# A new written order for all engines of a four-layer graph network kernel

## The chip, the cores and the metric

The kernel runs on one core of a Trainium2 chip. The metric is the device time of one execution in microseconds, as the median over runs. Below, PE is TensorE (matmuls), DVE is VectorE, ACT is ScalarE, POOL is GpSimd and SP is SyncE, which only issues DMA transfers.

## The reference

The input x is a batch of 128 matrices of 128 nodes by 512 features in float32; adj is one 128 x 128 matrix. Four layers follow each other, each as x = layernorm(x + layer(x)):

```python
# layer 0
y   = einsum('nm,bmd->bnd', adj, x);  out = y @ weight + bias
# layer 1
q, k, v = x @ Wq.T, x @ Wk.T, x @ Wv.T
rel = adj.T * (q @ k.T);  rel = rel / norm(rel, axis=2);  out = rel @ v
# layer 2
h   = x @ W;  s1, s2 = h @ a1, h @ a2
e   = leaky_relu(s1[:, :, None] + s2[:, None, :]) * adj
out = elu(softmax(e) @ h + beta * h)
# layer 3
pre = (adj @ x)[:, :, None, :] + ((adj @ x + b) - adj @ x)[:, :, :, None]
out = max(relu(pre), axis=-1)
```

## The kernel before, in words

**Groups and stages.** The batch is cut into NG = 32 groups of G = 4 matrices. A group is one tile of 128 partitions x 4 x 512. The layers are pipelined over the groups: while TensorE works on layer 0 of group g (tiles named y), it also works on layer 1 of group g-1 (m, rel, v, o) and layer 2 of group g-2 (z), with layer 3 of the group before that (p_a). In the steady state every period holds the same steps for successive groups.

**The four big products.** In each group there are four products of a [512 x 512] left side with a [512 x 512] weight: y with the weight of layer 0, x with the product of Wq and Wk (m), x with Wv (v), and z with the weight of layer 2. Each is done by the Strassen-Winograd scheme in seven block products instead of eight (`product`, line 533; the products are numbered 1 to 7, `ORDER`, `REGION` and `BLOCK` say in which order, in which PSUM region and for which block). In most groups the block products 2 and 4 are done by the same scheme once more, on 128 x 128 blocks (`inner_product`, line 498), in three steps each: products 1, 2 and 5, then 6 and 3, then 7 and 4 (`SMALL`). Both inner products of one big product share two PSUM banks with tag pi. An inner step writes into a bank only when VectorE has read the earlier step's result of that bank. So there are three kinds of names: r_y, r_m, r_v, r_z are results of plain block products (256 columns a matmul), pi_y, pi_m, pi_v, pi_z those of inner ones (128 columns), and p_y, p_z, p_rel, p_o, p_a are the small products with adj, the attention or the scores.

**Who does what.** The sums of left blocks that the scheme needs, s_y, s_x, s_z for the outer and si_y, si_x, si_z for the inner level, are made by GpSimd (`left_factors`, line 358). The results are added into the tiles x (layer 0), tT (scores), v and c (layer 2) by VectorE, some are copied by ScalarE. Transposes of activations into yT and zT come out of p_y and p_z by ScalarE copies; xT, relT and eT are made by VectorE's block transposes (xB, relB, eB) and DMA transfers on SP's queue. The normalisation (`norm`, line 615) takes statistics on VectorE (`stats`: BN statistics and their aggregation), ve on VectorE, rstd = ve^(-1/2) on GpSimd, nmean on VectorE and the scaling of x by ScalarE. In layer 2, s1 and s2 are dot products on VectorE; s2 goes through DRAM and comes back spread over the partitions (s), and then VectorE makes e<-s,d and the leaky step e<-e, two steps with both operands in SBUF, GpSimd multiplies by adj, VectorE takes the maximum, ScalarE the exponential, VectorE divides and adds beta (four steps).

**What sets the order.** Each step is not run where it is written but recorded with a number:

```python
def emit(at, f, *args):
    pieces.append((at, lambda: f(*args)))
...
for _, f in sorted(pieces, key=lambda p: p[0]):
    f()
```

The steps run in the order of these numbers, and the class InOrder (line 18) keeps each engine's instructions in that order. All instructions are issued from InOrder's helper, so all have line L26 in the profile. A step's number is 28 x group plus a value of `TABLE` (`times`). `FIRST` replaces values for groups 0 and 1 and `LAST` for the last three groups; `STEPS` gives, relative to the start of a big product, when each block product and each inner step begins and when its result is read. The scale is only an order: nothing waits for a point of time. What waits is decided by semaphores, for data and for buffers.

Of the kernel before, what the change touches and what calls it, by code (L numbers as in the profile page):

```python
# [10 lines left out]
ALU = mybir.AluOpType  # L11
# [18 lines left out]
def kernel(  # L30
# [215 lines left out]
    def row(at, step, n=G):  # L246
# [4 lines left out]
        load=[-23.2169], y=[0.4502, 1.7198, 2.5377, 4.2529],  # L251
        y_sums=[5.3577, 5.4124, 7.8235, 8.8388], y_inner=[6.5498, 7.664, 8.3588, 9.0762],
        y_w=[6.7589, 7.6588, 8.3277, 16.9708, 16.9901, 20.5607, 22.7653],
        stats0=[13.328, 13.6989, 14.9332, 14.6913], norm0=[15.5628],
        apply0=[17.0291, 17.8869, 17.7334, 18.253], turn=[16.7073, 16.2021, 14.9969, 20.612],
        turn_blocks=[17.8971, 18.3579, 19.2263, 19.3554],
        move=[20.4296, 21.0211, 24.5297, 21.5216], x_sums=[25.5005, 25.8871, 27.6629, 27.0652],
        x_inner=[27.1832, 28.0762, 28.1744, 27.3808],
        m=[27.6814, 29.311, 30.5193, 32.9685, 32.6007, 32.3909, 36.4113],
        scores=[35.7913, 36.5286, 36.9062, 39.5258], masked=[40.2], squares=[41.6744],  # L260
        turn_rel=[40.7045], move_rel=[40.942, 41.4556, 41.6809, 42.7864], inverse=[42.997],
        v=[41.1715, 38.9562, 41.2808, 38.8925, 41.0631, 48.9771, 50.8054],
        attend=[51.0766, 51.9776, 54.2466, 53.0567], residual=[51.4403, 53.0619, 54.4101, 55.0641],
        squares1=[51.8389, 54.8288, 55.7527, 55.9297], dots=[52.2629, 53.9621, 54.8819, 55.6838],
        norm1=[56.0324], scale=[57.2146], apply1=[65.5539, 65.7375, 66.5847, 65.6302],
        spread=[58.597], leaky=[61.9353], weighted=[63.694], greatest=[63.7], exps=[64.3087],
        divide=[64.7559], turn_att=[67.1344], with_beta=[64.8337], turn_blocks_2=[64.9823],
        move_2=[66.4103], gather=[70.2679, 71.1247, 73.2155, 74.6156],
        z_sums=[75.1661, 76.1025, 77.0322, 77.3655], z_inner=[76.1384, 77.0913, 77.9699, 79.3217],
        z_w=[76.5003, 77.2488, 83.0675, 84.5887, 83.8747, 83.1527, 86.1311],  # L270
        exp=[85.3247, 85.2563, 97.2575, 99.4893], elu=[86.3247, 87.0299, 97.3808, 99.5574],
        norm2=[101.3033], apply2=[101.8904, 102.4013, 101.9063, 102.7223],
        widen=[104.0541, 104.4241, 105.8654, 107.0522],
        top=[104.3944, 105.3458, 106.4158, 107.431], norm3=[107.8979],
        apply3=[108.3981, 108.8547, 108.4952, 109.5013], store=[110.1315],
# [4 lines left out]
            y=[0.3837, 1.3837, 2.675, 3.675], y_sums=[5.7775, 6.2775, 7.2553, 7.6358],  # L280
            y_w=[6.8732, 7.6921, 8.8732, 9.8732, 10.8732, 11.5739, 12.3292],
            stats0=[14.4311, 14.4511, 14.4711, 14.4911], norm0=[15.816],
            m=[27.9566, 28.8805, 29.1757, 30.7027, 31.7537, 33.399, 33.5276],
            scores=[35.8497, 37.2073, 38.2073, 39.2073], masked=[39.9091], squares=[40.2891],
            turn_rel=[40.3993], move_rel=[42.0292, 41.2824, 41.094, 41.4824],
            v=[41.5081, 42.8089, 44.1636, 45.1636, 46.1636, 46.9988, 48.1636],
            attend=[50.6594, 51.5743, 52.6759, 53.6594], residual=[51, 52, 52.7256, 54.3006],
            squares1=[51.1766, 54.1407, 54.0138, 54.8004], norm1=[55.4948],
            apply0=[16.9376, 17.4687, 18.2447, 17.3632], turn=[18.8709, 20.6961, 20.9961, 21.4413],
            dots=[57.8, 58.1728, 59.9, 60.8223], scale=[61.2], spread=[61.7187], leaky=[62.1],  # L290
            weighted=[62.9], greatest=[64.0022], exps=[64.0333], divide=[65.5939],
            turn_blocks_2=[65.6], move_2=[65.65],
        ),
        1: dict(
            y=[-9.5161, -9.1442, -8.9161, -8.6161], y_sums=[-3.9496, -3.8496, -3.7496, -0.3469],
            y_w=[6.782, 7.7109, 8.6136, 9.601, 10.8116, 11.7295, 12.4613],
            stats0=[14.434, 14.5716, 15.1787, 15.3716], norm0=[16.6316],
            attend=[49.7, 52.43, 53.8336, 54.02], apply0=[18.7873, 19.43, 18.9743, 19.0873],
            turn=[20.5431, 20.6, 20.9, 21.2], x_sums=[22.1338, 23.4592, 24.0133, 26.9575],
# [5 lines left out]
            exp=[1.911, 11.611, 13.6093, 22.0992], elu=[5.6806, 13.5806, 18.6837, 22.1806],  # L305
            norm2=[23.3538], apply2=[24.522, 25.322, 26.3798, 26.0092],
            squares3=[34.1015, 35.8608, 35.7015, 37.144],
            widen=[43.9865, 55.4735, 53.8545, 58.1545], top=[45.1541, 57.9003, 58.5754, 60.4402],
            norm3=[64.2098], apply3=[66.5259, 66.9597, 67.9456, 68.5597], store=[69],
        ),  # L310
        NG - 2: dict(
            scale=[4.2], apply1=[4.5, 5.3942, 6.3, 6.1139], spread=[6.9011], leaky=[7.4],
            weighted=[9], greatest=[10.9571], exps=[12.8968], divide=[14.9407], turn_att=[18.5691],
            with_beta=[19.6], gather=[33.3301, 34.4633, 35.0947, 36.2151],
            z_sums=[37.1312, 37.1799, 37.2299, 38.9411],
            z_w=[37.2, 39.2089, 41, 42.6626, 44.8626, 46.5626, 48.2373],
            exp=[50.3972, 50.8866, 52.8866, 55.5591], elu=[52.4416, 54.6916, 59.5187, 64.5381],
            norm2=[65.7882], apply2=[67.872, 68.672, 69.472, 70.2058],
            widen=[73.03, 68.9544, 73.2544, 75.7764], top=[73.9203, 74.6682, 75.9682, 77.4682],
            stats3=[70.2144, 73.2078, 72.4861, 72.0071], norm3=[75.9789],  # L320
            apply3=[78.882, 79.8, 80.9786, 81.3657], store=[85.9721],
        ),
        NG - 1: dict(
            load_w2=[-23.6669], m=[-1.0871, 0.5618, 2.2887, 4.0287, 7.6759, 7.9287, 9.6287],
            scores=[12.8205, 13.6, 14.5, 15.7481], masked=[15.9045], squares=[16.4941],
            turn_rel=[17.4768], inverse=[19],
            v=[16.8753, 18.5753, 20.8511, 22.2355, 24.5079, 25.8571, 28.3688],
            attend=[28.9525, 29.7018, 30.5618, 31.4218], residual=[30.4, 31.27, 32.14, 33.01],
            stats1=[33.9, 34.2915, 34.1, 34.2], norm1=[34.3934],
            dots=[35.0895, 36.4469, 36.5469, 40.2922], scale=[42.7],  # L330
            apply1=[39.4587, 40.2587, 44.5045, 41.8587], spread=[43.4886], leaky=[44.7702],
            weighted=[46.0349], greatest=[48.0816], exps=[48.1871, 48.7343, 49.3109, 49.9109],
            divide=[48.5065, 49.3785, 49.9, 50.5], turn_att=[49.6131, 50.2131, 50.8131, 51.4131],
            with_beta=[49.934, 50.6249, 51.134, 51.6586],
            gather=[50.9668, 52.0102, 55.557, 62.8965], z_w=[52.2222, 56.5222, 60.615, 64.3222],
            exp=[55.264, 59.8536, 64.1536, 67.7536], elu=[55.3119, 60.4986, 66.3119, 69.7119],
            norm2=[57.5244, 62.8236, 67.713, 71.113], apply2=[59.9822, 65.342, 70.78, 74.4822],
            widen=[62.5511, 69.3064, 73.7305, 76.6387],
            stats3=[61.0987, 66.6487, 74.0987, 75.9582], norm3=[62, 67.45, 74.2351, 76.6],
            top=[69.7698, 73.416, 75.4098, 76.9098], apply3=[70.5171, 74.3, 76.4, 78],  # L340
            store=[73.5499, 75.2, 76.6055, 78.2055],
# [76 lines left out]
    def by_columns(p, a, b, first):  # L418

        for c in range(2):  # L420
            for k in range(2):
# [19 lines left out]


    STEPS = {
        "m": (
            {
                1: (0.0547, 0.3858),
                6: (1.5064, 1.6818),
                7: (2.8763, 2.9047),
                5: (4.4211, 5.0801),
                3: (5.9851, 6.5109),  # L450
            },
            {
                2: ((1.231, 1.341), (2.5246, 2.879), (4.1971, 4.3926)),
                4: ((4.0286, 4.2384), (5.2415, 5.786), (6.8079, 8.6144)),
            },
        ),
        "0": (
            {
                1: (-0.2799, 0.7512),
                6: (1.3262, 1.5837),  # L460
                7: (3.3936, 3.4058),
                5: (4.5192, 5.2093),
                3: (6.2408, 6.2609),
            },
            {
                2: ((0.7436, 1.3293), (2.4284, 2.8511), (4.032, 5.0699)),
                4: ((3.4633, 4.0434), (5.1574, 5.9066), (6.5107, 6.8625)),
            },
        ),
# [802 lines left out]
```

## Time and profile before

| | |
|---|---|
| median of 3 runs | 2172.33 us (2172.3 to 2172.41) |
| profiled execution | 2172.45 us |
| its span in the trace | 2170.2 us |
| granted TensorE clock | 0.998 |
| PE / DVE / ACT / POOL busy | 98% / 82% / 59% / 45% of the span |
| DMA | 139.67 MB, mean 64 GB/s |

The profile was taken in one execution. The span is what the engines' records cover, the execution's own time is 2.25 us longer. A row of the timeline gives the start, the busy time, the engine, the operation, the tile that is written and the tiles that are read, and in square brackets the idle time of the engine before it with what ended it. A matmul in float32 counts as two records in the trace. The ends of matmuls are modelled from their size, so a row's busy time can overlap the next row's start, and the distance of starts is the better measure.

### The profile page before, as it was taken

Reading aid. Unit: us, or ns where it says so; the run is one execution under the profiler, and the core shown is the slowest. Engines: PE = TensorE matmul, PEld = TensorE weight load, DVE = VectorE, ACT = ScalarE, POOL = GpSimd, SP = SyncE. Lnnn points to the kernel's source line nnn. Section 1 sums busy time; section 2 is a strip of 40 time slices with the busy share of each in tenths; the row PEclk is TensorE's granted clock in tenths of the full one; section 3 lists DMA queues with packets and bytes.
Section 4 is the critical chain, followed back from the end, with each engine's and each line's share of the span. In section 5 each row is a group of like instructions: output and inputs, shape, how many; then the busy total and the mean of one; then the engine's idle time right before and its main releaser. Section 6 shows DMA issues by size and latency. Waiting matters only on the chain.

```text
span 2170.2 us, 36980 instructions
## 1 busy us (share of the span) xinstructions
PE 2123.9 (98%) x12325; PEld 1838.2 (85%) x12325; DVE 1784.4 (82%) x4961; ACT 1289.7 (59%) x2950; POOL 971.8 (45%) x949
## 2 busy tenths in 40 slices
PE   9999999999999999999999999999999999999996
PEld 7788888888888888888888888888888888888883
DVE  5688888888888888888888888888888788888887
ACT  3335566665566665566665566655666655676655
POOL 4244454444454444553544554444544445535431
PEclk9999999999999999999999999999999999999999
DMA  4012232222232222322222322312222213232201
GB/s 171 25 35 50 68 74 69 54 65 57 73 70 74 54 58 60 75 67 66 67 52 67 73 69 54 72 52 71 71 73 54 58 60 76 67 72 61 53 26 59
DMA packets 362526, 139.67 MB, mean 64 GB/s; under 512 B 303200, under 2 KB 318688, under 8 KB 362336
## 3 DMA queue, kind: packets, MB, share of 16 engines
q1 hardware_dynamic: 361808, 136.27, 24.9%
q8 instruction: 98, 1.61, 0.3%
q10 hardware_dynamic: 528, 1.05, 0.1%
q14 instruction: 92, 0.75, 0.1%
HBM read 56.17 MB, written 41.48 MB: 45 GB/s over the span
## 4 chain that ended last, share of the span: by engine, by line
PE 78%; DVE 9%; POOL 9%; issue 2%; ACT 1%; DMA 0%; SPq 0%; DVEq 0%; POOLq 0%; ACTq 0%
PE r_v L26 13%; PE r_z L26 12%; PE r_m L26 10%; PE r_y L26 6%; PE p_z L26 5%; PE p_y L26 5%; PE p_o L26 5%; PE p_a L26 5%; PE pi_v L26 4%; POOL s_y L26 4%; PE pi_z L26 4%; PE pi_m L26 3%; DVE x L26 3%; POOL si_y L26 3%; PE pi_y L26 2%
## 5 line engine op out<-in xcount | busy, mean ns | idle before, releaser
L26 ACT ACTIVATE x<-x,nmean,rstd 128x512 f32<-128x512 f32 x384 | 286.1, 811 | 95.8 <-DVE nmean L26 95.7
L26 ACT ACTIVATE scr<-x 128x512 f32<-128x512 f32 x360 | 225.7, 627 | 131.6 <-DVE x L26 128.8
L26 POOL TENSOR_TENSOR rn<-n,mhalf 128x4 f32<-128x4 f32 x32 | 33.0, 1030 | 374.8 <-ACT sq L26 374.8
L26 POOL TENSOR_TENSOR rstd<-ve,mhalf 128x4 f32<-128x4 f32 (+1 forms) x99 | 98.2, 992 | 228.5 <-DVE ve L26 227.5
L26 DVE SCALAR_TENSOR_TENSOR scr<-x,wa 128x512 f32<-128x512 f32 x256 | 175.0, 684 | 5.6
L26 DVE TENSOR_REDUCE mx<-p_a 128x1 f32<-128x512 f32 x128 | 88.0, 688 | 100.8 <-PE p_a L26 100.8
L26 ACT COPY v<-r_v 128x512 f32<-128x512 f32 x128 | 71.4, 582 | 160.1 <-PE r_v L26 160.1
L26 DVE TENSOR_TENSOR tT<-pi_m,tT 128x128 f32<-128x128 f32 x420 | 121.2, 306 | 54.3 <-PE pi_m L26 47.8
L26 POOL TENSOR_TENSOR s_y<-yT 128x512 f32<-128x512 f32 x32 | 40.6, 1267 | 249.1 <-ACT yT L26 249.1
L26 DVE TENSOR_TENSOR x<-r_y,x 128x512 f32<-128x512 f32 x194 | 129.8, 682 | 19.5 <-PE r_y L26 17.4
L26 PE MATMUL p_a<-x,adjT 128*128 128x512 f32 x256 | 131.8, 601 | 5.9 <-ACT x L26 4.2
L26 PEld LDWEIGHTS p_z<-eT,x 128*128 128x128 f32 x1024 | 131.6, 192 | 6.5 <-DVE x L26 0.8
L26 PE MATMUL p_y<-adjT,x 128*128 128x128 f32 x1024 | 134.5, 275 | 0.4 <-DMA x<-in_x_dram 0.4
L26 PE MATMUL p_z<-eT,x 128*128 128x128 f32 x1024 | 134.8, 275 | 0.0
L26 ACT COPY yT<-p_y 128x512 f32<-128x512 f32 x128 | 74.9, 585 | 100.2 <-PE p_y L26 100.2
L26 DVE TENSOR_TENSOR c<-pi_z,c 128x128 f32<-128x128 f32 x420 | 124.0, 307 | 11.3 <-PE pi_z L26 2.4
L26 PEld LDWEIGHTS p_y<-adjT,x 128*128 128x128 f32 x1024 | 129.1, 192 | 3.8 <-issue 0.5
L26 PE MATMUL p_o<-v,relT 128*128 128x512 f32 x256 | 130.7, 595 | 0.3 <-ACT xT L26 0.2
L26 PEld LDWEIGHTS p_rel<-xT,tT 128*128 128x128 f32 x1024 | 127.0, 192 | 3.4
L26 PE MATMUL p_rel<-xT,tT 128*128 128x128 f32 x1024 | 129.7, 275 | 0.0
L26 DVE TENSOR_TENSOR x<-pi_y,x 128x128 f32<-128x128 f32 x420 | 120.8, 306 | 9.4
L26 DVE TENSOR_TENSOR v<-pi_v,v 128x128 f32<-128x128 f32 x420 | 119.2, 302 | 6.2
(244 smaller groups left out, 6130.9 us busy)
## 6 DMA issues: line engine op xcount, KB each, us to landing
out_dram<-x SPq DMA_DIRECT2D x128, 256.0 KB, 2.1
x<-in_x_dram SPq DMA_DIRECT2D x31, 1024.0 KB, 7.4
xT<-xB SPq DMA_DIRECT2D x480, 64.0 KB, 2.3
relT<-relB SPq DMA_DIRECT2D x496, 16.0 KB, 1.8
eBd<-eB SPq DMA_DIRECT2D x30, 256.0 KB, 2.0
eT<-eBd SPq DMA_DIRECT2D x120, 64.0 KB, 2.0
s<-s2d SPq DMA_DIRECT2D x29, 256.0 KB, 5.2
w_sb<-in_L_gnn_weight_dram ACTq DMA_DIRECT2D x1, 1024.0 KB, 5.9
```

The lines of the kernel that those rows point to most:

```text
L26: return lambda *args, **kw: self.tc.keep_in_program_order(op(*args, **kw))
```

## The change

Only numbers change: the values of `TABLE`, `FIRST`, `LAST` and `STEPS`, and the lists of numbers handed to `emit`, `each`, `weight_blocks`, `left_factors` and `product` at the end of the function. Every engine runs the same instructions as before, in another order, with the same tiles and the same number of buffers. Counted out over a period of the steady state, the largest moves are these:

- p_y of blocks 1 to 3 and their copies into yT come earlier among the m products; the last r_m and pi_m pieces of group g-1 then follow them.
- GpSimd's order of a group's left sums is: s_y, s_y, si_y, then e x adj, yT, s_y, si_y, yT, si_y (before: s_y, s_y, si_y, si_y, e x adj, yT, si_y, s_y, yT). VectorE's e<-s,d and leaky step come after the first three.
- The inner steps and block products of y, m, v and z interleave differently (`STEPS`), so also the reads on VectorE.
- rstd of layer 1 moves behind the x sums on GpSimd. In the statistics of layer 0, block 3's come before block 2's as they did, with other steps between; nmean of layer 2 stands directly behind the step that GpSimd's rstd waits for (before, five adds of v stood between), as nmean of layer 0 stood and stands behind its own, apart from two adds of v.
- GpSimd's z sums run s_z, s_z, zT, si_z (before: s_z, s_z, si_z, zT).
- In the first groups the preparation of weights is placed anew, and products 7, 4, 3 of group 0 replace 7, 3, 4. In the last three groups the order of VectorE's, ScalarE's and TensorE's steps is shuffled within a few steps.

```diff
     TABLE = dict(
-        load=[-23.2169], y=[0.4502, 1.7198, 2.5377, 4.2529],
-        y_sums=[5.3577, 5.4124, 7.8235, 8.8388], y_inner=[6.5498, 7.664, 8.3588, 9.0762],
-        y_w=[6.7589, 7.6588, 8.3277, 16.9708, 16.9901, 20.5607, 22.7653],
-        stats0=[13.328, 13.6989, 14.9332, 14.6913], norm0=[15.5628],
-        apply0=[17.0291, 17.8869, 17.7334, 18.253], turn=[16.7073, 16.2021, 14.9969, 20.612],
+        load=[-21.1232], y=[0.9608, 1.8251, 2.1487, 2.7922],
+        y_sums=[4.5561, 5.0639, 6.7629, 6.9969], y_inner=[5.2833, 7.5035, 7.9599, 7.7423],
+        y_w=[6.4865, 10.1067, 9.7011, 18.5098, 16.5578, 25.5346, 18.8593],
+        stats0=[13.0727, 13.9676, 15.6348, 14.8804], norm0=[15.6928],
+        apply0=[16.441, 16.56, 17.1055, 18.4252], turn=[16.9531, 18.9169, 15.0983, 23.7872],
...
-        spread=[58.597], leaky=[61.9353], weighted=[63.694], greatest=[63.7], exps=[64.3087],
-        divide=[64.7559], turn_att=[67.1344], with_beta=[64.8337], turn_blocks_2=[64.9823],
-        move_2=[66.4103], gather=[70.2679, 71.1247, 73.2155, 74.6156],
-        z_sums=[75.1661, 76.1025, 77.0322, 77.3655], z_inner=[76.1384, 77.0913, 77.9699, 79.3217],
+        spread=[61.4852], leaky=[62.1614], weighted=[62.3481], greatest=[63.6868], exps=[63.9389],
+        divide=[64.6743], turn_att=[66.48], with_beta=[55.7842], turn_blocks_2=[65.0697],
+        move_2=[65.6032], gather=[70.1205, 71.0446, 73.2368, 74.4083],
+        z_sums=[74.7466, 74.9675, 75.3471, 79.5091], z_inner=[76.2873, 76.452, 76.7576, 79.7843],
...
-        norm2=[101.3033], apply2=[101.8904, 102.4013, 101.9063, 102.7223],
+        norm2=[100.4793], apply2=[101.1271, 102.2, 101.6434, 101.6261],
...
     STEPS = {
...
         "0": (
             {
-                1: (-0.2799, 0.7512),
-                6: (1.3262, 1.5837),
-                7: (3.3936, 3.4058),
-                5: (4.5192, 5.2093),
-                3: (6.2408, 6.2609),
+                1: (-0.2886, 1.0861),
+                6: (1.2661, 2.3878),
+                7: (3.1719, 4.2315),
+                5: (4.092, 4.8012),
+                3: (5.8133, 6.3959),
             },
             {
-                2: ((0.7436, 1.3293), (2.4284, 2.8511), (4.032, 5.0699)),
-                4: ((3.4633, 4.0434), (5.1574, 5.9066), (6.5107, 6.8625)),
+                2: ((0.925, 1.543), (2.5418, 3.9993), (4.5688, 5.5801)),
+                4: ((3.0391, 3.7075), (5.0748, 5.9439), (6.0353, 6.4062)),
             },
         ),
```

`STEPS` for "m", "v" and "2" and the remaining values of `TABLE`, `FIRST`, `LAST` and the lists at the end change in the same manner.

## The prediction

> **What bounds the kernel now.** I read the page's busy times first, then one window of the steady state, then the waits, then the timelines of TensorE, GpSimd and VectorE around the two places that the waits name. Page, then windows (length, then busy us of PE, PEld, DVE, ACT, POOL):
>
> ```profile
> PE 2123.9 (98%) x12325; PEld 1838.2 (85%) x12325; DVE 1784.4 (82%) x4961; ACT 1289.7 (59%) x2950; POOL 971.8 (45%) x949
> ...
> 1020.00:1088.00 68.00, 67.35 (x402) 59.00 (x401) 57.06 (x166) 42.36 (x98) 31.41 (x31) 1.00 0.25 63
> 2108.00:2170.20 62.20, 43.96 (x155) 25.82 (x153) 50.38 (x144) 34.92 (x67) 14.77 (x17) 0.92 0.13 51
> ```
>
> TensorE sets the pace for all but the last 60 us, where VectorE does (busy 9.3 to 9.4 us in each 10 from 2130 on). Only its gaps can be won. The steady ones are of two kinds only (waits: us in total, times, longest):
>
> ```profile
> PEld pi_y L26 <- POOL si_y L26: 14.5, 29, 0.6
> ...
> PE pi_y L26 <- DVE x L26: 9.7, 29, 0.3
> ...
> PE pi_y L26 <- POOL si_y L26: 8.9, 29, 0.4
> ```
>
> Timeline of TensorE in group 15 (start, busy, count of records; idle before in brackets):
>
> ```profile
> 969.34 0.61 PE L26 MATMUL pi_y<-w_sb,yT 128*128 128x128 f32 x4
> 970.25 0.49 PE L26 MATMUL pi_y<-u,si_y 128*128 128x128 f32 x2 [0.30 <-POOL si_y L26]
> 970.58 1.06 PE L26 MATMUL p_rel<-xT,tT 128*128 128x128 f32 x8
> ...
> 973.20 1.95 PE L26 MATMUL p_rel<-xT,tT 128*128 128x128 f32 x16
> 974.98 0.39 PE L26 MATMUL pi_y<-u,si_y 128*128 128x128 f32 x2
> ...
> 977.60 0.39 PE L26 MATMUL pi_y<-u,si_y 128*128 128x128 f32 x2
> 978.32 0.68 PE L26 MATMUL pi_y<-u,yT 128*128 128x128 f32 x4 [0.33 <-DVE x L26]
> 978.84 1.89 PE L26 MATMUL r_y<-w_sb,s_y 128*128 128x256 f32 x8
> ```
>
> Pitch: 16 records from 973.20 to 974.98 are 0.111 each (a product 128 wide is two records, 0.222; one 256 wide 0.432, one 512 wide 0.86). After 969.34 + 4 x 0.111 = 969.78 the next should start; it starts at 970.25, 0.47 late, and its two records take 0.33 instead of 0.22. The second: due 977.82, starts 978.32, 0.50 late, then 0.52 instead of 0.44. Together 0.47 + 0.11 + 0.50 + 0.08 = 1.16 us per group; the bracketed idle is smaller because ends are modelled. Cross-check: si_y comes 30 times from 113.6 to 2022.1, a period of 65.81 us; one group's products (48 of 0.222; 8 of 0.86; in each of four big products 20 of 0.432 and 14 of 0.222) are 64.6, and 64.6 + 1.16 is that period. So 29 x 1.16 = 33.6 us is all that the steady state can give back.
>
> Why si_y is late, GpSimd and then VectorE:
>
> ```profile
> 967.20 1.86 POOL L26 TENSOR_TENSOR s_y<-s_y,yT 128x512 f32<-128x512 f32 x1
> 969.02 1.17 POOL L26 TENSOR_TENSOR si_y<-yT 128x256 f32<-128x256 f32 x1
> 970.27 0.73 POOL L26 TENSOR_TENSOR si_y<-si_y,yT 128x256 f32<-128x256 f32 x1
> ...
> 966.17 1.81 DVE L26 TENSOR_TENSOR e<-s,d 128x512 f32<-128x512 f32 x1
> 968.01 1.59 DVE L26 SCALAR_TENSOR_TENSOR e<-e 128x512 f32<-128x512 f32 x1
> ```
>
> The same sums elsewhere take 1.27 and 0.73, the e steps at least 1.08 and 0.69: VectorE and GpSimd take turns.
>
> **What the Trainium skill says.** "SBUF — State Buffer", section "Who interferes with whom": a VectorE instruction with two SBUF inputs and a GpSimd instruction that reads SBUF exclude each other for a whole instruction; ScalarE and TensorE have ports of their own. The trace agrees: 1.86 against 1.27, 1.17 against 0.73, 1.81 against 1.08, and steps with a PSUM operand keep their length. "Perfetto Trace Analysis", section "GPSIMD Engine Instruction": spans there are unreliable, starts are to be used. Here the difference is small: s_y 1.27, spacing about 1.35 for the first.
>
> **The change, part by part.** No instruction is added or removed, so the sum is made of waits only. "Matmul time" is TensorE's own time between two points if it never waits, counted from the new order with the pitches above.
>
> *Stall 1.* Before, 4.79 us of matmul time lie between the last p_y and the first pi_y<-u,si_y, and 4.79 + 0.47 = 5.26 was needed. After, p_y of block 3 stands earlier, with its ScalarE copy, and 8.93 lie between; the m products that it overtakes end later, and the scores p_rel, which need them, keep 0.6. Needed without hold-up: eviction 0.3 + 0.58, s_y 1.35 + 1.3, si_y 0.75 = 4.3. Slack 4.6; even held as before it holds. Both e steps of VectorE now follow these sums. Gain 0.47 + 0.11.
>
> *Stall 2.* The third pi_y step reuses the bank of the second. Before, 2.40 us of matmul time lay between, 2.90 were needed; after, 4.13. Gain 0.50 + 0.08. What is late next: VectorE's read of r_y after product 6 now queues behind the reciprocal and the four e steps, which wait for the landing of s (5.2 us). I get a read end 0.1 to 0.2 before product 7 is due; a landing 0.5 later would stall 0.4. GpSimd's last si_y/yT before the second pi_y step has 0.2 to 0.6.
>
> *New waits around norm0.* VectorE's nmean of layer 2 now stands directly behind its ve (before, five v adds lay between), as that of layer 0 stood already behind ve and two v adds; each time VectorE waits up to 1 us for GpSimd's rstd (1.01). Counting VectorE's queue from the last y add in positions of matmul time (r_v's first product at 0): two adds to 1.5, four statistics of 0.8, four x3 steps of 0.69 and three v adds of 0.28 bring ve to 8.4, rstd to 9.5, nmean after it, the second pair to 11.1, xB 0.65, three v adds 0.9: the bank is free at 12.7 to 12.8, and TensorE wants it at 12.7. I take 0.1 plus 0.1 of restart; 0 to 0.6 is open. Behind the second nmean also stand ScalarE's x3 steps and zT copies; the last zT ends at about 15.6, and GpSimd's new order s_z, s_z, zT, si_z (1.35 + 1.25 + 1.25 + 0.75; before, si_z came third) ends at 20.2, TensorE wants si_z at 20.1, 0.2 late with its latency of 0.1; the slip above covers half. I take 0.4 per group for all new waits, 0 below and 1.0 above as bounds.
>
> *Moved without cost.* rstd of layer 1 goes behind all x sums on GpSimd: the x sums gain 1 us, the 16 xT transfers start about 1.4 us later and still land ahead (si_x slack some 3 us). SP's queue keeps its rows; the x load stands 2.1 of 28 slots later, still most of a period ahead of its use. If that cover were gone, m products would wait 1 us per group.
>
> *Start-up.* TensorE's gaps from 10 to 170 us sum to 9.7. Products 7 and 4 go ahead of 3 in group 0, so that two evictions lie beside it (a gap of 1.46 at 61.7 goes); other gaps may grow. I take -2, bounds -5 and +2.
>
> *Tail.* Same VectorE-bound work, shuffled; one nmean there waits 0.6 for rstd, one PE wait of similar size goes. I take 0, bounds -2 and +2.
>
> Sum: 29 x (0.4 - 1.16) = -22, -2, 0: about -24. Profiled execution 2172.45 (span 2170.2 and 2.25 around it), the median 2172.33, so they are interchangeable: 2172.4 - 24 = 2148.5. I predict 2149.
>
> **Rivals.**
> (a) As worked out, 54%: 2142 to 2156 (0.15 to 0.6 of new waits per group).
> (b) The new waits are covered, 22%: 2172.4 - 33.6 - 2 = 2137, 2135 to 2142. For it: TensorE's 29 equal gaps are the only steady ones, and my new ones are within 0.2 of nothing. Against: several have that slack at once.
> (c) A new wait takes the old ones' place, 15%: the chain through both rstd comes 0.8 later than worked out, or the s landing moves the e chain by 0.6 and r_y stalls: 0.9 to 1.1 per group, 2163 to 2172.
> (d) Slower, 9%: VectorE's queue stands behind GpSimd's pow twice, and with it ScalarE's x and zT, GpSimd's z sums. From 1.3 us lateness of that one chain on, what it costs exceeds 1.16 and the 2 us of start-up; at 1.8 it is 29 x 0.6 = +17: 2188. For it: the waits of before already have nmean on rstd 33 times, up to 1.1 us, and ScalarE's x on nmean for 95.7 us in all; against: GpSimd is 45% busy and has nothing else queued there in the new order.
> That the change doesn't do what it says is excluded: the new order of p_y and of the e steps can be counted.
>
> **How the numbers follow.** 0.2% is 4.3 us, about what a measurement can tell from no change. (a), (b) and the lower half of (c), 0.08, are faster; within 0.2% (2168 to 2176.7) falls the upper half of (c), 0.07; (d) is slower, 0.09. The range leaves out the lower end of (b) (0.05), the top of (c) (0.04) and (d): 2136 to 2170; case (a) alone 2142 to 2156.
>
> **What would show it.** Right: no wait of pi_y on si_y or x of 29 times; first s_y sums 1.27 and si_y 0.73; a si_y period of 65.1 (64.6 for b). New rows in the waits, 29 times each, of pi_v on v or pi_z on si_z, and nmean on rstd with two waits of about 1 us per group. Wrong: a period of 65.5 or more, r_y waiting for x, or TensorE waiting for v over 0.6 at a time.

## The result and the profile after

The changed kernel takes 2141.59 us (median of 4 runs, 2141.52 to 2141.63), beside 2172.32 us of the kernel before on the same chip. The ratio is 0.9859, with a 95% interval of 0.9842 to 0.9876: it is faster by 1.4%, or 30.7 us. The forecast was 2149, with a range of 2136 to 2170; the measured time lies just below case (a) (2142 to 2156) and within case (b) (2135 to 2142), at its upper end.

The page of the kernel after, busy times and the chain that ended last, then that chain before:

```profile
PE 2116.7 (99%) x12325; PEld 1836.7 (86%) x12325; DVE 1725.1 (81%) x4961; ACT 1293.5 (60%) x2950; POOL 954.3 (45%) x949
...
PE 94%; DVE 3%; SPq 1%; DMA 1%; POOL 0%; issue 0%; ACT 0%; ACTq 0%; DVEq 0%; POOLq 0%
...
PE 78%; DVE 9%; POOL 9%; issue 2%; ACT 1%; DMA 0%; SPq 0%; DVEq 0%; POOLq 0%; ACTq 0%
```

Before, PE had 78% of that chain, DVE and POOL 9% each. Now it is PE's nearly alone. VectorE's busy time is 59 us smaller (1784.4 to 1725.1) with the same instructions: a step that is held up by a step of the other engine counts as busy in the profile, so a hold-up that goes shows as less busy time, not as less idle time.

The waits view has no row in which pi_y waits for si_y or for x any more. Some waits of the other engines have grown. The one that the prediction named is this (us in total, times, longest; before 21.4, 33, 1.1):

```profile
DVE nmean L26 <- POOL rstd L26: 54.5, 63, 1.1
```

Timeline of group 16's y sums, first GpSimd, then VectorE, then TensorE:

```profile
1010.27 1.71 POOL L26 TENSOR_TENSOR s_y<-yT 128x512 f32<-128x512 f32 x1 [2.99 <-ACT yT L26]
1012.06 1.27 POOL L26 TENSOR_TENSOR s_y<-s_y,yT 128x512 f32<-128x512 f32 x1
1013.29 0.72 POOL L26 TENSOR_TENSOR si_y<-yT 128x256 f32<-128x256 f32 x1
...
1015.40 1.06 DVE L26 TENSOR_TENSOR e<-s,d 128x512 f32<-128x512 f32 x1
1016.50 0.69 DVE L26 SCALAR_TENSOR_TENSOR e<-e 128x512 f32<-128x512 f32 x1
...
1017.97 0.61 PE L26 MATMUL pi_y<-w_sb,yT 128*128 128x128 f32 x4
1018.42 0.39 PE L26 MATMUL pi_y<-u,si_y 128*128 128x128 f32 x2
```

The first si_y starts at 1013.29, is done 0.72 later, and TensorE wants it at 1018.42: 4.4 us to spare. The e steps start after these three sums and take 1.06 and 0.69, where they took 1.81 and 1.59. The first s_y is still held (1.71 instead of 1.27): VectorE's step x<-m,x of layer 2, which reads two tiles in SBUF, runs from 1010.16 to 1010.85 beside it. It costs nothing here.

What is left of TensorE's steady waits are restarts: an instruction starts on time or nearly so, and its second record comes about 0.1 us late. TensorE's timeline at three places of the period, and at the first of them ScalarE's copy that frees the bank:

```profile
1008.75 0.59 ACT L26 COPY tT<-r_m 128x512 f32<-128x512 f32 x1
1009.41 1.98 PE L26 MATMUL r_m<-s_x,t_m 128*128 128x256 f32 x8
...
1043.85 1.05 PE L26 MATMUL p_z<-eT,x 128*128 128x128 f32 x8
1044.76 0.49 PE L26 MATMUL pi_v<-u_v,si_x 128*128 128x128 f32 x2
1045.08 0.39 PE L26 MATMUL pi_v<-t_v,si_x 128*128 128x128 f32 x2
...
1051.80 0.61 PE L26 MATMUL pi_z<-w_sb,zT 128*128 128x128 f32 x4
1052.24 0.48 PE L26 MATMUL pi_z<-u,si_z 128*128 128x128 f32 x2
1052.56 1.02 PE L26 MATMUL p_a<-x,adjT 128*128 128x512 f32 x2
```

pi_v was due at 1043.85 + 8 x 0.111 = 1044.74 and starts at 1044.76; its two records then take 0.32 instead of 0.22. pi_z starts on time, at 1052.24, and also takes 0.32. These two are the places that the prediction named. The third, at an r_m product, it did not name: ScalarE's copy ends at 1009.34, r_m starts on time at 1009.41, and the next product starts at 1011.23, 0.09 late. VectorE's queue ahead of pi_v is the one that the prediction worked out:

```profile
1041.36 0.16 DVE L26 SCALAR_TENSOR_TENSOR nmean<-mv,rstd 128x4 f32<-128x4 f32 x1 [0.60 <-POOL rstd L26]
...
1043.11 0.16 DVE L26 SCALAR_TENSOR_TENSOR nmean<-mean,rstd 128x4 f32<-128x4 f32 x1 [1.12 <-POOL rstd L26]
1043.29 0.71 DVE L26 STREAM_TRANSPOSE xB<-x 128x512 f32<-128x512 f32 x1
1043.93 0.78 DVE L26 TENSOR_TENSOR v<-pi_v,v 128x128 f32<-128x128 f32 x3
```

**Where the 30.7 us come from.** The period of the steady state is taken below as the mean distance of the starts of e x adj on GpSimd over 20 groups in the middle of the trace: 65.82 before, 64.94 after. 29 x 0.88 = 25.5 us. TensorE's gaps in the first 180 us, taken from the distances of starts, sum to 15.5 before and 10.0 after: 5.5. Behind 2050 us its gaps are 0.9 smaller, but from the end of its last matmul to the end of the span 11.6 pass instead of 10.6, so the tail gives nothing. Together 31, where the spans say 30.5 (2170.2 to 2139.7): the windows cut the stages only roughly. The runs on the start-up and the tail below give 4.9 and 0.5, and with 25.5 that is 30.9.

### The profile page after: what moved, and what is told of

Same layout as the page of the kernel before. It is cut to its first block, busy times and chain, and to the rows that moved or that the text cites. A ratio compares the mean times of both kernels' runs of the same rounds, so it can differ in the third digit from the quotient of the medians.

```text
span 2139.7 us, 36859 instructions
## 1 busy us (share of the span) xinstructions
PE 2116.7 (99%) x12325; PEld 1836.7 (86%) x12325; DVE 1725.1 (81%) x4961; ACT 1293.5 (60%) x2950; POOL 954.3 (45%) x949
## 3 DMA queue, kind: packets, MB, share of 16 engines
q10 hardware_dynamic: 528, 1.05, 0.2%
## 4 chain that ended last, share of the span: by engine, by line
PE 94%; DVE 3%; SPq 1%; DMA 1%; POOL 0%; issue 0%; ACT 0%; ACTq 0%; DVEq 0%; POOLq 0%
PE r_m L26 13%; PE r_y L26 13%; PE r_v L26 12%; PE r_z L26 12%; PE p_rel L26 5%; PE p_y L26 5%; PE p_o L26 5%; PE p_z L26 5%; PE p_a L26 5%; PE pi_m L26 4%; PE pi_y L26 4%; PE pi_z L26 4%; PE pi_v L26 4%; SPq L26 1%; DVE x L26 1%; DVE st L26 1%
## 5 line engine op out<-in xcount | busy, mean ns | idle before, releaser
L26 DVE SCALAR_TENSOR_TENSOR x<-p_o,rn,x 128x512 f32<-128x512 f32 x128 | 95.4, 745 | 58.4 <-PE p_o L26 58.1
L26 ACT COPY r_y<-bias_sb 128x512 f32<-128x512 f32 x64 | 38.0, 593 | 161.4 <-DVE tT L26 161.3
L26 POOL TENSOR_TENSOR s_x<-xT 128x512 f32<-128x512 f32 x64 | 80.6, 1280 | 121.5 <-DMA xT<-xB 73.1
L26 PE MATMUL p_y<-adjT,x 128*128 128x128 f32 x1024 | 129.9, 275 | 0.5 <-DMA x<-in_x_dram 0.5
L26 PEld LDWEIGHTS p_y<-adjT,x 128*128 128x128 f32 x1024 | 124.5, 192 | 2.4 <-issue 0.7
L26 PE MATMUL p_o<-v,relT 128*128 128x512 f32 x256 | 125.7, 594 | 0.3 <-ACT xT L26 0.2
L26 PE MATMUL r_m<-s_x,t_m 128*128 128x256 f32 x512 | 123.7, 384 | 0.0
```

The costliest lines, as they stand in the source:

```text
L26: return lambda *args, **kw: self.tc.keep_in_program_order(op(*args, **kw))
```

## The experiments

Each ratio is taken to the kernel before on the same chip; its median there lay between 2171.77 and 2172.16. The 95% intervals of the ratios are about 0.15% (3 us) to each side, so a difference of 2 us between two runs rests on the single executions and on the traces. Three questions were open: whether the two stalls of the period have one cause or two, what the cause is, and what the rest of the new order gives.

### Is it the hold-up? The e steps later, p_y where it was

```diff
-        leaky=[61.9353]
+        leaky=[63.52]
```

> The kernel before with one number changed: VectorE's e<-s,d and leaky step stand behind the first add of r_y, about 3.6 us later, p_y stays where it was. Theory (hold-up): the second s_y takes 1.27 and the first si_y 0.73 instead of 1.86 and 1.17, so that si_y is ready about 0.5 before TensorE wants it, and the first wait on si_y is gone. Rival (GpSimd is late only because p_y is): the wait on si_y stays at 0.47. The whole time is no test here, as GpSimd's e x adj and all behind it come later: 2160 to 2200 for both.

Measured: 2192.04, one run. The time was no test; the first sums are. GpSimd, then TensorE:

```profile
975.37 1.27 POOL L26 TENSOR_TENSOR s_y<-s_y,yT 128x512 f32<-128x512 f32 x1
976.59 0.73 POOL L26 TENSOR_TENSOR si_y<-yT 128x256 f32<-128x256 f32 x1
...
977.51 0.61 PE L26 MATMUL pi_y<-w_sb,yT 128*128 128x128 f32 x4
977.95 0.39 PE L26 MATMUL pi_y<-u,si_y 128*128 128x128 f32 x2
...
987.18 0.68 PE L26 MATMUL pi_y<-u,yT 128*128 128x128 f32 x4 [0.68 <-DVE x L26]
```

One number moves both e steps. With p_y in its old place, s_y takes 1.27 and si_y 0.73, and pi_y<-u,si_y starts at 977.95 = 977.51 + 4 x 0.111: the first stall is gone. So the first stall came from the hold-up and not from the place of p_y alone. The second stall grew (about 0.84 instead of 0.50), and r_y waits for x as well, because VectorE's e chain comes later.

### One part alone: p_y earlier

```diff
-        y=[0.4502, 1.7198, 2.5377, 4.2529]
+        y=[0.4502, 1.7198, 2.1487, 2.7922]
```

> The kernel before with one part of the change: p_y of blocks 2 and 3 stand earlier among the m products (7.64 us of matmul time instead of 4.79 before the first pi_y step on si_y). Theory (two stalls, each with its own cause): the wait on si_y goes, 0.58 us per group, the other stays: 2172.3 - 29 x 0.58 = 2155.5. Rival (the second stall is set by VectorE's queue behind the transfer of s and the e steps, at a fixed time): TensorE arrives 0.58 earlier at the second stall and waits 0.58 longer there: 2172, with pi_y on x at about 1.1 us a time.

Measured: 2153.91 (2153.79 to 2154.02), ratio 0.9918 (0.9903 to 0.9933). The number is close to the first theory's 2155.5, by luck: the reason is another. **Both** stalls of pi_y are gone, and there is a new one. TensorE, then VectorE:

```profile
1021.67 0.39 PE L26 MATMUL pi_m<-si_x,t_m 128*128 128x128 f32 x2
1022.39 1.99 PE L26 MATMUL r_m<-s_x,m_qk 128*128 128x256 f32 x8 [0.34 <-DVE tT L26]
...
1022.78 1.06 DVE L26 TENSOR_TENSOR e<-s,d 128x512 f32<-128x512 f32 x1
1023.87 1.05 DVE L26 SCALAR_TENSOR_TENSOR e<-e 128x512 f32<-128x512 f32 x1
```

r_m is due at 1021.67 + 0.222 = 1021.89 and starts at 1022.39, 0.50 late, plus 0.10 of restart. Before, p_y of block 3 stood between the r_m products 5 and 3 and gave VectorE 0.9 us to read the bank that they share; taken away from there it leaves that read uncovered. The steady part is 65.82 - 65.24 = 0.58 per group: 1.18 won, 0.60 lost.

### The other part alone, and both: the third pi_y step later

```diff
-                2: ((0.7436, 1.3293), (2.4284, 2.8511), (4.032, 5.0699)),
+                2: ((0.7436, 1.3293), (2.4284, 2.8511), (4.6, 5.0699)),
```

> The kernel before with another part alone: the third step of the inner y product 2 is moved behind the four r_y products, so that 4.13 us instead of 2.40 lie between the two uses of its bank. Both theories: the wait on x goes, the wait on si_y stays: 2172.3 - 29 x 0.58 = 2155.5. If the bank is not the cause but VectorE's lateness in general, another TensorE wait of about 0.5 per group appears behind it: 2170.

Measured: 2166.36 (2166.13 to 2166.45), ratio 0.9975 (0.9965 to 0.9985), a third of what was expected. The wait on x went, but the moved step had covered something else, the read between the r_y products 5 and 3:

```profile
978.54 0.39 PE L26 MATMUL pi_y<-t,si_y 128*128 128x128 f32 x2
979.02 1.99 PE L26 MATMUL r_y<-w_sb,s_y 128*128 128x256 f32 x8
```

r_y is due at 978.76, starts 0.26 late and loses 0.10 more. The expectation had named such a wait, though with 0.5.

> Both parts of the two runs before together, everything else as before. Theory: both stalls gone and nothing new, as the order in norm0 and of the z sums is the old one: 2172.3 - 33.6 = 2138.7. Rival (freed TensorE time is taken back by a new wait in the same period, as the change has at pi_v): 2145 to 2155.

Measured: 2164.66 (2164.45 to 2164.84), ratio 0.9967 (0.9955 to 0.998). Worse than the first part alone: both new waits are there (0.60 at r_m and 0.36 at r_y), and as p_y alone had ended both old stalls, the second part could only cost. The theory that each stall needs its own part of the change falls here.

### One move for both stalls: p_y earlier, with the cover of r_m kept

This adds to the p_y edit one moved product, so that the first r_y product lies between the two uses of the r_m bank; the third pi_y step stays where it was.

```diff
-        y=[0.4502, 1.7198, 2.5377, 4.2529]
+        y=[0.4502, 1.7198, 2.1487, 2.7922]
...
-                3: (5.9851, 6.5109),
+                3: (6.8, 7.0),
```

> The kernel before with p_y of blocks 2 and 3 earlier (as in the first run) and, in addition, the r_m product 3 behind the first r_y product, so that VectorE's read of the r_m bank is covered by 1.73 us of matmul time again. Theory (both stalls of before come from one hold-up, and the first run only lost a cover): no steady wait of TensorE is left, 2171.8 - 29 x 1.16 = 2138. Rival (the earlier p_y shifts the hold-up on, the next bank waits): 2150 to 2160, with pi_y on x or p_rel on tT in the waits.

Measured: 2139.29 (2138.28 to 2140.3), ratio 0.985 (0.9835 to 0.9864). Three moved steps, p_y of two blocks and one r_m product with its read, do what the whole new order does. The four executions fall into two pairs, 2138.28 and 2138.47, 2140.1 and 2140.3; the trace is of the slowest, and what the pairs differ by is open. The window of the steady state, then GpSimd, VectorE and TensorE:

```profile
1020.00:1088.00 68.00, 68.00 (x410) 59.93 (x409) 55.99 (x160) 41.23 (x96) 33.20 (x34) 1.00 0.25 63
...
1016.79 1.27 POOL L26 TENSOR_TENSOR s_y<-s_y,yT 128x512 f32<-128x512 f32 x1
...
1018.82 1.44 POOL L26 TENSOR_TENSOR si_y<-si_y,yT 128x256 f32<-128x256 f32 x1
1020.88 1.27 POOL L26 TENSOR_TENSOR e<-e,adj_sb 128x512 f32<-128x512 f32 x1 [0.63 <-DVE e L26]
...
1019.75 1.05 DVE L26 SCALAR_TENSOR_TENSOR e<-e 128x512 f32<-128x512 f32 x1
...
1025.98 1.14 DVE L26 SCALAR_TENSOR_TENSOR e<-e,rs,beta_i 128x128 f32<-128x128 f32 x4
...
1027.83 0.60 DVE L26 TENSOR_TENSOR x<-pi_y,x 128x128 f32<-128x128 f32 x2
...
1026.75 0.39 PE L26 MATMUL pi_y<-u,si_y 128*128 128x128 f32 x2
...
1029.59 0.61 PE L26 MATMUL pi_y<-u,yT 128*128 128x128 f32 x4
```

No steady wait is left; the period is 64.64, which is TensorE's work. The same steps in the kernel before, GpSimd and VectorE:

```profile
970.96 1.27 POOL L26 TENSOR_TENSOR e<-e,adj_sb 128x512 f32<-128x512 f32 x1
...
972.26 0.69 DVE L26 TENSOR_REDUCE nm<-e 128x4 f32<-128x512 f32 x1 [1.45 <-POOL e L26]
...
975.04 1.81 DVE L26 SCALAR_TENSOR_TENSOR e<-e,rs,beta_i 128x128 f32<-128x128 f32 x4
...
977.57 0.61 DVE L26 TENSOR_TENSOR x<-pi_y,x 128x128 f32<-128x128 f32 x2
```

From the start of the second pi_y step to that of the third TensorE still has 29.59 - 26.75 = 2.84 us, as before. VectorE's read of the bank ends 28.43 - 26.75 = 1.68 after the second step's start; before, it ended 3.20 after it (977.57 + 0.61 - 974.98). The way of these 1.52 us goes over GpSimd. The read stands behind the four divisions on VectorE. These need ScalarE's exponentials, which need VectorE's maximum nm, which needs GpSimd's e x adj, and e x adj stands behind the y sums in GpSimd's queue. Before, the leaky step ended at 968.01 + 1.59 = 969.60, but GpSimd was busy with the sums until 971.00, and VectorE waited 1.45 for e x adj. Now e x adj starts right behind the leaky step, which ends at 1020.80. Counted from the second pi_y step, e x adj starts 1.85 earlier than before, the divisions start 0.83 earlier (975.04 - 974.98 = 0.06 after it before, 26.75 - 25.98 = 0.77 ahead of it now), and they take 1.14 instead of 1.81, 0.67 less, as they are hardly held by GpSimd's next sums any more. 0.83 + 0.67 = 1.50. The 0.83 alone are more than the 0.50 that was missing.

So the second stall came from the same late y sums as the first. What made them late enough for it is not separated: with p_y earlier the second s_y starts 2.18 earlier against the second pi_y step (967.20 - 974.98 and 1016.79 - 1026.75), and the hold-up on GpSimd is smaller too. It has not gone: the leaky step still takes 1.05 instead of 0.69, and the second si_y 1.44 instead of 0.73. An estimate from the trace of before: the held s_y and si_y cost GpSimd 0.59 + 0.44 = 1.03 us ahead of e x adj, more than the 0.50 of the second stall, so the hold-up alone could account for it. No run takes away the hold-up and leaves p_y and the e steps where they are.

### Undo p_y in the changed kernel

Block 3's p_y and the two sums behind it go back:

```diff
-        y=[0.9608, 1.8251, 2.1487, 2.7922]
-        y_sums=[4.5561, 5.0639, 6.7629, 6.9969]
+        y=[0.9608, 1.8251, 2.1487, 5.1]
+        y_sums=[5.11, 5.15, 6.7629, 6.9969]
```

> The changed kernel with p_y of block 3 put back among the m products (4.13 us of matmul time before the first pi_y step on si_y, instead of 8.93), VectorE's order untouched. Theory (hold-up): the y sums meet the e steps again and need 5.26, so TensorE waits 1.1 and 0.1 per group: 2141.6 + 29 x 1.2 = 2176. Rival (no hold-up in the new order, as the e steps stand elsewhere on VectorE): 4.3 are needed, a wait of 0.2 and 0.1: 2150.

Measured: 2217.75 (2217.69 to 2217.94), ratio 1.021 (1.0195 to 1.0225): 76 us more than the changed kernel, more than either theory. GpSimd, ScalarE and TensorE:

```profile
1052.12 1.86 POOL L26 TENSOR_TENSOR s_y<-s_y,yT 128x512 f32<-128x512 f32 x1
1053.93 1.18 POOL L26 TENSOR_TENSOR si_y<-yT 128x256 f32<-128x256 f32 x1
...
1050.11 0.58 ACT L26 COPY yT<-p_y 128x512 f32<-128x512 f32 x1 [2.04 <-PE p_y L26]
1050.59 0.60 ACT L26 COPY r_y<-bias_sb 128x512 f32<-128x512 f32 x1
...
1050.13 0.39 PE L26 MATMUL pi_m<-si_x,t_m 128*128 128x128 f32 x2
1051.24 1.99 PE L26 MATMUL r_y<-w_sb,yT 128*128 128x256 f32 x8 [0.72 <-ACT r_y L26]
```

The hold-up is back, within 0.01 of its old size (1.86 and 1.18), with VectorE's order untouched, so the new order avoids it by p_y's place. But the stall is not where it was expected: the bias copy that r_y needs stands behind the late yT copy on ScalarE, so r_y waits 0.89 + 0.10 first, which is most of the time that si_y needs. Then an r_m product lost its cover by p_y and waits 0.88 + 0.10 for ScalarE's copy, and the second pi_y step waits 0.45 + 0.10 for si_y. These are 2.5 us of the period's 67.52 - 64.94 = 2.58. The run shows the hold-up and its place, not its price: p_y carried three covers.

### Start-up and tail

The old numbers of the first two groups and of the weights' preparation, and then those of the last three groups, in the changed kernel:

> The changed kernel with the old numbers for the first two groups and for the preparation of the weights. The sum in the prediction took 2 us for the start-up: 2143.6. TensorE's gaps in the first 180 us of the two traces differ by 5.5, of which one is the second group's own stall pair and so not undone here: 2146. If the start-up is hidden behind something else: 2141.6.

Measured: 2146.46 (2146.29 to 2146.8), ratio 0.9882 (0.9867 to 0.9897). The start-up's own new order is worth 4.9 us.

> The changed kernel with the old numbers for the last three groups. Prediction: nothing, 2141.6 within 2. From the traces: TensorE's gaps behind 2050 us are 0.9 smaller after, the stretch behind its last matmul 1.4 longer: the old tail would be 0.5 faster, 2141.1.

Measured: 2142.14 (2141.84 to 2142.79), ratio 0.9862 (0.9848 to 0.9877). The tail's new order is worth 0.5 at most, within what these runs can tell. In the traces it gives nothing: the stretch behind the last matmul is 1.0 longer after, and not 1.4 as the expectation has it.

### What is left in the changed kernel

xB of block 0 behind the three adds of v, and si_z ahead of zT:

```diff
-        turn_blocks=[17.6387, 18.378, 19.3199, 18.8892]
+        turn_blocks=[17.85, 18.378, 19.3199, 18.8892]
-        z_inner=[76.2873, 76.452, 76.7576, 79.7843]
+        z_inner=[75.2, 76.452, 76.7576, 79.7843]
```

> The changed kernel with the two small waits that it brought taken out: xB of block 0 stands behind the three v adds on VectorE (0.65 earlier bank), and si_z stands before zT on GpSimd (1.25 earlier). Theory (they are what is left of the 0.24 us per group over the floor): 2141.6 - 29 x (0.12 + 0.09) = 2135.5. Rival (the 0.1 of restart is no wait but part of these steps): 2141 to 2142.

Measured: 2139.31 (2138.88 to 2139.51), ratio 0.9849 (0.9833 to 0.9866): 2.3 us instead of 6.1. The restarts at pi_v and pi_z are gone, which refutes the rival, but a new one of 0.13 stands at p_a in each group, where TensorE now comes earlier than VectorE's maximum leaves the bank, and the one at r_m stays. The period goes from 64.94 to 64.87. The next run moved that maximum:

```diff
-        top=[104.9696, 105.5877, 105.8825, 107.7194]
+        top=[102.95, 105.5877, 105.8825, 107.7194]
```

> The changed kernel without its two small waits (as in the run on pi_v and si_z), and with the first maximum of p_a between two xB steps on VectorE, about 1.1 us earlier, since in that run p_a came to wait for it by 0.1 at the restart. Theory: 29 x 0.1 less than that run, 2139.3 - 2.9 = 2136.4. Rival (ScalarE's queue, whose top step stands earlier too, gives it back): 2139 or more.

Measured: 2139.84 (2139.58 to 2141.7), ratio 0.9852 (0.9835 to 0.9868), no gain. The wait at p_a went, and in about ten of the groups the first pi_m step on si_x now waits, up to 1.2 us a time. The trace is of the slowest of the four executions (2141.7; the others 2139.58 to 2140.06), so the others may have fewer of these waits. The likely way, argued and not tested, is over xB, which the maximum pushed back and which starts the transfers that feed si_x. The cause named by the rival, ScalarE, does not show as lost time of TensorE.

### A version that beats both

The three moved steps with the changed kernel's start-up:

> The same with the changed kernel's numbers for the first two groups and the weights' preparation. The run that took these away from the changed kernel lost 4.9 us; if the two gains add up, 4.9 below the run before it in this list: 2133 by the theory. Rival (the start-up's gain needs the new order of the whole): no lower than that run.

Measured: 2137.18 (2137.0 to 2137.22), ratio 0.984 (0.9825 to 0.9854), 4.4 below the changed kernel (4.1 when each is taken against the kernel before on its chip) and 2.1 below the run with the old start-up. The intervals of the ratios overlap, but all four executions lie below all of those two kernels. The gains do not add up in full. By the spans of the two traces the new start-up gives 3.2 here, against 4.9 in the changed kernel. In this run TensorE waits 3.19 us at 110 us for VectorE's d of group 0; with the old start-up it waited 2.5 at the same step (110.16 + 0.22 to 112.85), so this explains 0.7 and the rest is open. The last run moved group 0's e steps back to cover that:

```diff
-            spread=[61.7827], leaky=[62.1], weighted=[62.205], greatest=[64.0362], exps=[64.0854], divide=[65.2555], turn_blocks_2=[65.6]
+            spread=[62.6], leaky=[62.65], weighted=[64.37], greatest=[64.38], exps=[64.39], divide=[65.9], turn_blocks_2=[66]
```

> The version with three moved steps and the new start-up, with the e steps of group 0 (transposes of d, e, e x adj, maximum, exponential, division) behind the first r_y and r_m products of group 2. In the run without this TensorE waited 3.19 us once, at 110 us, for VectorE's d. Theory: the wait is covered by 3.7 us of matmul time and nothing else comes: 2137.2 - 3.2 = 2134. Rival (the later e steps of group 0 hold up VectorE's reads or GpSimd's sums of group 2 by as much): 2136 to 2138.

Measured: 2137.1 (2136.98 to 2137.28), ratio 0.984 (0.9824 to 0.9857): the same. Three new waits took the place of the one:

```profile
109.88 1.99 PE L26 MATMUL r_m<-s_x,m_qk 128*128 128x256 f32 x8 [0.68 <-DVE tT L26]
115.12 0.71 PE L26 MATMUL p_rel<-xT,tT 128*128 128x128 f32 x4 [0.99 <-DVE tT L26]
126.24 2.00 PE L26 MATMUL r_y<-w_sb,s_y 128*128 128x256 f32 x8 [0.39 <-DVE x L26]
```

## Why the prediction was right, and where it was not

- **The bound and the prize.** Right. The period fell from 65.82 towards TensorE's own work, which was put at 64.6 and is 64.64 in the run without a steady wait.
- **Stall 1.** Right in the mechanism and the size. The hold-up made si_y late: it goes with p_y in place when the e steps move, and comes back within 0.01 when p_y is put back in the new order.
- **Stall 2.** The gain came, the cause was wrong. The step said that the third pi_y step gains by standing 4.13 instead of 2.40 us behind the second. In the kernel before that distance is not needed: with it left at 2.40 and p_y earlier the stall went, because VectorE's read comes 1.52 earlier. I had taken the late y sums as what TensorE waits for, and had not followed them to the e x adj that stands behind them on GpSimd, and from there to VectorE's read of the bank. The prediction survived since the change did both. For the p_y move alone the same reading gave 2155.5, and 2153.91 came only because a new wait of 0.60 took what the second stall gave. In the changed kernel itself the distance was not tested. There the four divisions are still held (1.80), and the reads of the bank end at 1026.22, 2.73 after the second step's start at 1023.49; with 2.84 to the third step that would be just in time.
- **New waits around norm0.** The chain was right in place and time: the bank came free 0.02 late, si_z on time, nmean waited twice. The size, 0.4 per group, is 64.94 - 64.64 = 0.30. Of this pi_v and pi_z are 0.2; the restart at r_m, 0.09, was not foreseen.
- **Read of r_y behind the e chain.** It does not show as a wait in the changed kernel; the slack of 0.1 to 0.2 held.
- **Start-up.** The mis-sized term: 2 was taken; the run gave 4.9 and the gaps 5.5, at the end of the bound of 5. I had priced only the gap at 61.7, which is gone, and took the rest as even.
- **Tail.** Taken as nothing, and nothing is what the traces and the run can tell.
- **The sum.** 29 x (0.30 - 1.18) = -25.5, about -5 and 0, against -22, -2 and 0. Steady state and start-up each gave about 3 more, so the time lies at the edge of case (a). That case's limits are also about 1 us too high for its own terms: 2172.4 - 2 - 29 x (1.16 - 0.15) = 2141, and with 0.6 it is 2154. Of the marks that I had set, two failed. The first s_y is 1.71 and not 1.27, held by another step. And the waits show no 29 rows of pi_v on v or pi_z on si_z: a restart leaves next to no idle time, and is seen only in the distances of starts.

## What to carry to other kernels

Follow a late step down every queue that it stands in. Here GpSimd's late sums delayed TensorE directly and, through the e x adj that stood behind them, also VectorE's read of a bank: one lateness looked like two unrelated stalls with two releasers. Before a step is moved, ask what it covered where it stood; here a 0.9 us product between two uses of a bank was worth 0.6 a group. And when the steady state has two or three repeated waits, try the few moves that end them before a whole new order: three moved steps gave what rearranging all engines gave, 2139.29 against 2141.59.

## What the runs showed of the hardware

- A float32 matmul whose wait ends just in time still loses about 0.10 us: it starts on time, and its second record comes late (pi_z above: 0.00 late, then 0.32 for 0.22). With their producers moved earlier, the restarts at pi_v and pi_z went. In the steady state of the changed kernel this is most of what is left, 0.28 of 0.30 us per group at three places.
- A hold-up is shared out in both directions. In the kernel before, s_y 1.86 for 1.27, si_y 1.17 for 0.73, e 1.81 for 1.06 and the leaky step 1.59 for 0.69 alternate in one stretch: 0.59 + 0.44 + 0.75 + 0.90 = 2.7 us of held time on two engines from one overlap, all of it shown as busy.
